# Moving half of one chunk's depthwise convolution from TensorE to VectorE in a fused attention and mixture-of-experts kernel

## The chip, the cores and the metric

The kernel runs on one core of one Trainium2 chip. The metric is device time in microseconds (us) of one execution, from launch to end; the profile gives the span from the first to the last instruction of one such execution. The engines are called PE (TensorE, matmuls), PEld (its weight loads), DVE (VectorE), ACT (ScalarE), POOL (GpSimd) and SP (the queue that issues DMAs). All data are 32-bit floats.

## The reference

The input is 16 images of 256 channels with 64 x 64 pixels. Two layers follow each other, each as a residual.

```python
def layer0(xg):                      # xg: group norm of x, 32 groups
    xn = rmsnorm(xg, g_norm)         # over the channels
    q, k, v = w_qkv @ xn             # 4 heads of 32
    q = softmax(q, over head_dim); k = softmax(k, over pixels)
    context = k @ v.T; out = context.T @ (q * 32 ** -0.5)
    return rmsnorm(w_out @ out + b_out, g_out)

def layer1(xg):                      # xg: group norm of the new x
    prob = softmax((mean over pixels of xg) @ router_w.T / 2)
    for the two best of 4 experts:   # chosen per image, weights sum to 1
        h = gelu(depthwise 3x3 convolution of xg by dw[e] + dw_b[e])
        out += weight * (pw[e] @ h + pw_b[e])
    return out

x = x + layer0(group_norm(x)); x = x + layer1(group_norm(x))
```

## The kernel before

Every image passes through phases: "in" (statistics of the first norm), "q" (norm, transposes, projection, the sums for the attention context), "out" (attention output, its norm, the transpose back and the sum into the image), "route" (second norm, choice of experts) and "x" (the experts). Phases in, q and out run over 8 groups of 512 pixels; x runs over 4 chunks j of 16 rows (1024 pixels). Phases of neighbouring images overlap.

The order of all instructions is written out. Each step is entered with `at(phase, image, group, key, function)`, its place is the phase's start plus the slot times the group plus a number from the table `PLAN`, and all steps are sorted by place and emitted in that order (`rows.sort`, line 917). Each engine takes its instructions strictly in this order. The phase x has slots of 16 places, and one image has 64 places.

In phase x the 256 channels are split into two halves, for which the convolution is done in different ways.

- Channels 128 to 255, "the second half", go by DVE. `pad1` (line 693) writes the normed chunk with its border rows into one of two padded buffers `pd1`; `start1` (line 731) begins an accumulator "acc" on ACT with the first of nine taps; `tap1` (line 739) adds the other eight on DVE, 1024 pixels in one instruction; `gelu1` (line 746) writes the result "h". This is done for both chosen experts. There are two "acc" buffers.
- Channels 0 to 127, "the first half", go by PE. `pad0` (line 653) writes the chunk into `pd0` with even and odd rows and columns apart; `lay` (line 678) copies it to HBM; `spread` (line 683) reads it back so that 16 channels at a time, with their pixel neighbourhood, fill the 128 partitions; `conv0` (line 713) convolves both experts with two matmuls of 256 columns per group of 16 channels, 8 groups; `gelu0` (line 724) evacuates.

`pointwise` (line 752) multiplies by the chosen experts' weights. It fills four PSUM banks per chunk, one for each set q of pixels (even or odd row, even or odd column), and each bank holds two output halves m of 256 pixels. Parts 0 and 1 multiply "h" of the two experts at full depth of 128 (line 768). Parts 2 and 3 multiply the first half's result in four bands of 32 partitions (line 779, "banded")[...]. Part 4, used in the last image alone, adds the image itself by an identity matmul (line 774). `residual` (line 788) adds bank and bias into the image: on DVE (line 795), or on ACT in the last image (line 793), where the image is in the bank already. There are seven PSUM banks for all of this and one more for the context.

Other steps of which the prediction speaks: `out_norm` (line 456) scales the attention output on DVE (line 463), in the last image on ACT (line 461); `out_add` sums it into the image (line 477); `stats` (line 262) takes the first norm's statistics; `gn1_sums` (line 490) has one instruction per image at line 493; `pick_taps` (line 554) chooses the second half's taps; line 241 and 242 are the helper `rsqrt`, begun on DVE and ended on POOL; line 416 is a small matmul of the attention's weights. Two paths exist, and a check on the weights at the start selects the pipelined one (`pipelined_path`), which all traces here run.

Of the kernel before, what the change touches and what calls it, by code (L numbers as in the profile page):

```python
# [47 lines left out]
EARLY = 3  # L48
NRING = 7
# [4 lines left out]
    "load_x1": 2.47, "mean": 1.04, "means": 4.69, "dev": 5.07, "devs": 8.24, "scale": 8.52,  # L54
    "bias": 12.08, "in_lead": 22.23, "norm0": -5.91, "norm1": -3.77, "turn_x0": 0.61, "x_sq0": 1.9,
    "x_sq1": 2.11, "turn_x1": 1.64, "x_sq2": 2.36, "x_sq3": 2.68, "token": 3.59, "x_keep0": 5.41,
    "x_keep1": 5.42, "x_keep2": 5.2, "x_keep3": 5.22, "project0": 3.62, "evacuate0": 5.48,
    "project1": 4.85, "evacuate1": 5.69, "project2": 5.61, "evacuate2": 6.6, "project3": 5.69,
    "evacuate3": 6.83, "context": 7.87, "q_sum": 8.01, "q_norm": 13.4, "q_turn": 15.77,
    "q_keep": 16.04, "mix_a": 8.41, "mix_turn": 9.67, "mix_v": 10.33, "mix_vv": 11.49, "mix_b": 12,  # L60
    "mix_out": 12.87, "mix_c": 13.33, "mix_lead": 15.68, "attend0": -0.16, "out_sq0": 0.33,
    "out_sq1": 0.7, "out_scale0": 1.35, "out_norm0": 2.44, "attend1": 0.39, "out_sq2": 1.3,
    "out_sq3": 1.47, "out_scale1": 2.38, "out_norm1": 3.76, "out_turn0": 4.83, "out_add0": 6.02,
    "sq_sums0": 6.68, "out_turn1": 5.56, "out_add1": 6.85, "sq_sums1": 7.24, "sums1": 7.53,
    "means1": 7.77, "scale1": 8.7, "router": 9.48, "route": 9.99, "choose": 12.08,
    "pick_taps": 16.41, "route_lead": 22.29, "pick_rows0": 12.27, "pick_rows1": 15.38,
    "pick_row_bias": 13.7, "weigh": 19.29, "pick_bias": 20.19, "pick000": 1.5, "pick100": 11.76,
    "pick001": 2.67, "pick101": 11.83, "pick002": 5.78, "pick102": 15.2, "pick003": 8.9,
    "pick103": 15.49, "pick010": 1.98, "pick110": 13.36, "pick011": 3.58, "pick111": 15.09,
    "pick012": 4.61, "pick112": 15.41, "pick013": 6.8, "pick113": 16.18, "lay_pw": 10.27,  # L70
    "spread_pw": 12.95, "taps0": 6.17, "taps1": 1.71, "taps2": 2.27, "taps3": -4.16, "taps4": 9.52,
    "taps5": -1.21, "taps6": -1.21, "taps7": 11.56, "pad1": -10.11, "start0": -3.22, "tap01": 0.77,
    "tap02": 1.13, "tap03": 1.92, "tap04": 2.35, "tap05": 2.68, "tap06": 3.77, "tap07": 5.22,
    "tap08": 6.68, "gelu10": 10.88, "start1": 3.82, "tap11": 5.21, "tap12": 6.65, "tap13": 8.35,
    "tap14": 9.77, "tap15": 11.78, "tap16": 12.05, "tap17": 13.11, "tap18": 13.97, "gelu11": 15.52,
    "pad00": 1.66, "pad01": 2.92, "lay": 4.37, "spread0": 6.43, "conv0": 10.64, "gelu00": 11.57,
    "spread1": 6.19, "conv1": 11.39, "gelu01": 12.09, "spread2": 5.8, "conv2": 10.58,
    "gelu02": 11.06, "spread3": 6.79, "conv3": 12.01, "gelu03": 12.46, "spread4": 6.78,
    "conv4": 13.04, "gelu04": 14.02, "spread5": 7.96, "conv5": 13.16, "gelu05": 14.2,
    "spread6": 9.37, "conv6": 13.42, "gelu06": 14.64, "spread7": 10.33, "conv7": 13.97,  # L80
    "gelu07": 14.66, "pw00": 16.91, "pw01": 17.04, "pw02": 18.17, "pw03": 18.59, "pw10": 19.2,
    "pw11": 20.88, "pw12": 21.41, "pw13": 21.48, "residual00": 20.87, "residual01": 25.47,
    "residual02": 27.17, "residual03": 27.67, "store0": 29.36, "residual10": 23.57,
    "residual11": 25.64, "residual12": 27.45, "residual13": 28.04, "store1": 33.91,
    "in_first": 2.74, "in_more": 1.74, "q_first": 9.11, "out_first": 7.86, "out_more": 15.48,
    "q_less": 0.26, "load_a0": -16.2, "load_a1": -8.65, "load_b0": -17.65, "load_b1": -7.1,
    "stats0": -4.87, "stats1": -3.45, "load_weights": 21.49, "scale_weights": -2.89,
    "spread_taps00": -8.7, "spread_taps01": -1.56, "spread_taps10": 1.5, "spread_taps11": 5.1,
    "end_pw00": 16.45, "end_pw01": 18.13, "end_pw02": 14.45, "end_pw03": 15.46,
    "end_residual00": 23.47, "end_residual01": 25.21, "end_residual02": 26.09,  # L90
    "end_residual03": 28.08, "end_pw10": 17.51, "end_pw11": 19.09, "end_pw12": 14.97,
    "end_pw13": 16.08, "end_residual10": 28.63, "end_residual11": 28.83, "end_residual12": 29.05,
    "end_residual13": 30.35, "x_0": -0.07, "x_1": -0.03, "x_2": -0.04, "x_e1": -0.24, "x_e2": -0.02,
    "route_0": 1.22, "route_1": -0.07, "route_2": 0, "route_e1": 0.66, "route_e2": 0.04,
    "out_0": -0.91, "out_1": 0.05, "out_2": -0.02, "out_e1": 0.4, "out_e2": 0.22, "q_0": -0.72,
    "q_1": 1.29, "q_2": 0.04, "q_e1": -0.03, "q_e2": 0, "in_0": 8.12, "in_1": 4.22, "in_2": 0.93,
    "in_e1": 0.1, "in_e2": 0.11, "pw04": 19.17, "pw14": 23.02, "end_pw04": 18.16, "end_pw14": 20.35,
# [4 lines left out]
def pipelined_path(ctx, tc, ring, wqkv, x, w_outT, b_out, g_out, router_wT, router_b, dw, dw_b, pwT, pw_b, out):  # L102
# [79 lines left out]
    dww = const.tile([P, NE, 10], FP, name="dww")  # L182
# [7 lines left out]
    def load_weights():  # L190
# [5 lines left out]
        nc.sync.dma_start(out=dww[:, :, 0:9], in_=dw[P:C])  # L196
        nc.sync.dma_start(out=dww[:, :, 9:10], in_=dw_b[P:C])
# [63 lines left out]

    def stats(b, g, k):
        st = live["st", b] if ("st", b) in live else new(small, [P, KH, NG, 6], "st", b, bufs=2)
        nc.vector.bn_stats(st[:, k, g], live.pop(("xa", b, g, k)) if b else x1(b, g)[:, k])  # L264
# [191 lines left out]
    def out_norm(b, g, hf):  # L456
        ob = new(work, [P, 2, C], "ob", b, g, hf, bufs=3)
        s, po = live.pop(("s", b, g, hf)), live.pop(("po", b, g, hf))
        if b == NB - 1:
            for c in range(2):  # L460
                nc.scalar.activation(ob[:, c], po[:, c], AF.Copy, scale=s[:, c : c + 1])
        else:
            nc.vector.tensor_tensor(ob, po, s.unsqueeze(2).to_broadcast([P, 2, C]), ALU.mult)
# [90 lines left out]
    def pick_taps(b):  # L554

        oh, ds = live["oh", b], new(small, [P, TOPK, 10], "ds", b, bufs=2)
        for i in range(TOPK):
            dt = new(small, [P, 10, NE], "dt", b, i, bufs=2)
            nc.vector.tensor_tensor(
                dt, dww.rearrange("p e t -> p t e"),  # L560
                oh[:, i].unsqueeze(1).to_broadcast([P, 10, NE]), ALU.mult,
            )
            nc.vector.tensor_reduce(ds[:, i], dt, AX.X, ALU.add)
# [66 lines left out]
    def lay_pw(b):  # L630

        d = live["layp", b] = hbm.tile([P, TOPK * C], FP, tag="layp", name=f"layp_{b}")
        nc.sync.dma_start(out=d, in_=live.pop(("pw0", b)).rearrange("p i o -> p (i o)"))
# [18 lines left out]

    def pad0(b, j, s):
# [11 lines left out]
        if s == 0:  # L665
            if j == 0:
                nc.gpsimd.memset(pd0[:, 0, :, 0], 0.0)
            else:
                nc.gpsimd.tensor_copy(pd0[:, 0, :, 0], pd0[:, 0, :, QA])
        xs = x1c(b, j)[:, 0].rearrange("p (a s w) -> p a s w", s=2, w=W)  # L670
        put(1 - s, s, QA, xs[:, :, s])
# [11 lines left out]
    def spread(b, j, g):  # L683

        d, t = live["lay", b, j], new(work, [P, QA * PC], "xr", b, j, g, bufs=12)
        rows = d[g * CH : (g + 1) * CH].rearrange("c (v n) -> v c n", v=4)
        for a in range(2):
            nc.sync.dma_start(
                out=t[a * P // 2 : (a + 1) * P // 2],
                in_=rows[:, :, a * PC : (a + QA) * PC],  # L690
            )

    def pad1(b, j):

        t, prev = pd1[j % 2], pd1[(j + 1) % 2]
# [17 lines left out]
    def conv0(b, j, g):  # L713
        if g % 2 == 0:
            live["dw", b, j, g // 2] = bank("dw", b, j, g)
        po = live["dw", b, j, g // 2][:, g % 2 * GT // 2 : (g % 2 + 1) * GT // 2]
        rows3 = live["xr", b, j, g].rearrange("p (a w) -> p a w", w=PC)
# [6 lines left out]
    def gelu0(b, j, g):  # L724

        po = live["dw", b, j, g // 2][:, g % 2 * GT // 2 : (g % 2 + 1) * GT // 2]
        nc.scalar.activation(  # L727
            live["xr", b, j, g][:, 0 : GT // 2], po, AF.Gelu, bias=live["bv", b][:, g : g + 1]
        )

    def start1(b, j, i):
        ds = live["ds", b]
        acc = new(work, [P, QR, W], "acc", b, j, i)
        nc.scalar.activation(  # L734
            acc, pd1[j % 2][:, 0:QR, 0:W], AF.Identity,
            bias=ds[:, i, 9:10], scale=ds[:, i, 0:1],
        )

    def tap1(b, j, i, t):
        acc = live["acc", b, j, i]  # L740
        nc.vector.scalar_tensor_tensor(  # L741
            acc, pd1[j % 2][:, t // 3 : t // 3 + QR, t % 3 : t % 3 + W],
            live["ds", b][:, i, t : t + 1], acc, ALU.mult, ALU.add,
# [7 lines left out]

    def pointwise(b, j, m, part):


        ms = slice(m * P, (m + 1) * P)

        both = (b, j) == (NB - 1, NQ - 1)
        if ("ppw", b, j) not in live:
            live["ppw", b, j] = [bank("pw", b, j, q) for q in range(4)]
        group = ("parts", b, j, None if both else m)  # L760
        parts = live[group] = live.get(group, 0) + 1
        n = 5 if b == NB - 1 else 4
# [788 lines left out]
```

## Time and profile before

| what | value |
|---|---|
| median of 3 runs | 2724.32 us (2722.52 to 2724.56) |
| the profiled execution | 2722.39 us |
| its span, first to last instruction | 2720.7 us |
| mean granted TensorE clock | 0.992 |
| PE busy | 2636.2 us, 97% |
| PEld busy | 2257.1 us, 83% |
| DVE busy | 2417.5 us, 89% |
| ACT busy | 2083.4 us, 77% |
| POOL busy | 767.4 us, 28% |
| DMA | 394.77 MB, mean 145 GB/s |

Busy time is the time in which at least one instruction of the engine is recorded as running. Records of successive instructions overlap a little, so what one instruction costs its engine is better read from the start of one to the start of the next. In a row of the profile, `L741 DVE ... acc<-pd,ds,acc` names the line, the engine, and the tiles written and read.

### The profile page before, as it was taken

To read this page: it belongs to the slowest core of one execution; us is meant where nothing else is said; L and a number is where in the kernel's file an instruction comes from. 1 tells how busy PE (TensorE), PEld (TensorE's weight loads), DVE (VectorE), ACT (ScalarE), POOL (GpSimd) and SP (SyncE) were. 2 spreads that over 40 slices of the span, in tenths; PEclk is the share of its full clock that TensorE was granted. 3 is DMA by queue.
4 is the path that set the end of the run, shared out by engine and by line. 5 is a ranking of instruction groups with operands and counts; after the bars stand their busy time and mean duration, and the time that the engine had idled before them with its cause. 6 is when DMAs were issued, how large, how long until landed. Compare 5 with 4: busy or idle time off the path is not lost.

```text
span 2720.7 us, 55294 instructions
## 1 busy us (share of the span) xinstructions
PE 2636.2 (97%) x19300; PEld 2257.1 (83%) x19300; DVE 2417.5 (89%) x4480; ACT 2083.4 (77%) x5230; POOL 767.4 (28%) x874
## 2 busy tenths in 40 slices
PE   6898999999999999999999999999999999998888
PEld 5787888888888888888888888888888888886677
DVE  6889998999989898898989989898898988889984
ACT  3576788887887888788787888888788788876543
POOL 2242232322323222232322323233222323232200
PEclk9999999999999999999999999999999999999989
DMA  4335454454545546355354545445454443525332
GB/s 155 113 125 148 141 170 153 133 167 155 154 146 158 158 144 184 129 162 170 125 170 153 155 155 158 155 143 173 143 159 154 145 135 123 150 85 140 118 110 89
DMA packets 229711, 394.77 MB, mean 145 GB/s; under 512 B 25904, under 2 KB 108336, under 8 KB 229424
## 3 DMA queue, kind: packets, MB, share of 16 engines
q1 hardware_dynamic: 228880, 390.75, 46.4%
q8 instruction: 156, 2.56, 0.4%
q14 instruction: 131, 1.07, 0.1%
q10 hardware_dynamic: 544, 0.39, 0.0%
HBM read 280.82 MB, written 110.23 MB: 144 GB/s over the span
## 4 chain that ended last, share of the span: by engine, by line
PE 88%; DVE 7%; ACT 1%; issue 1%; DMA 1%; POOL 1%; SPq 0%; ACTq 0%; POOLq 0%; DVEq 0%
PE pw L779 17%; PE pw L768 16%; PE dw L719 15%; PE pq L346 14%; PE pc L364 8%; PE po L440 8%; PE px L315 4%; PE tr L468 4%; DVE acc L741 3%; PE ptq L387 2%; DMA ring<-in_x 1%; DVE ring L477 1%; DVE ring L795 1%; PE pw L774 1%; DVE st L264 0%
## 5 line engine op out<-in xcount | busy, mean ns | idle before, releaser
L741 DVE SCALAR_TENSOR_TENSOR acc<-pd,ds,acc 128x1024 f32<-128x1024 f32 x1024 | 1304.7, 1284 | 14.7 <-ACT acc L734 10.9
L242 POOL TENSOR_TENSOR s<-s,mhalf 128x2 f32<-128x2 f32 x256 | 212.2, 831 | 1103.2 <-DVE s L241 1085.4
L346 PE MATMUL pq<-wqkv_n,xg 128*128 128x256 f32 x2048 | 504.7, 384 | 0.9
L719 PE MATMUL dw<-xr,taps 128*128 128x256 f32 x2048 | 489.2, 381 | 8.4 <-ACT xr L727 6.2
L768 PE MATMUL pw<-h,pw 128*128 128x256 f32 x2048 | 480.7, 383 | 15.6 <-ACT h L750 10.0
L779 PE MATMUL pw<-xr,psp 32*128 32x256 f32 x8192 | 485.1, 382 | 0.0
L779 PEld LDWEIGHTS pw<-xr,psp 32*128 32x128 f32 x8192 | 405.9, 185 | 66.7 <-issue 47.3
L768 PEld LDWEIGHTS pw<-h,pw 128*128 128x128 f32 x2048 | 382.2, 191 | 74.3 <-ACT h L750 12.4
L719 PEld LDWEIGHTS dw<-xr,taps 128*128 128x128 f32 x2048 | 374.5, 190 | 58.9 <-ACT xr L727 11.4
L346 PEld LDWEIGHTS pq<-wqkv_n,xg 128*128 128x128 f32 x2048 | 370.8, 192 | 58.2 <-ACT xt L333 11.7
L322 ACT ACTIVATE jx<-px 128x256 f32<-128x256 f32 x512 | 195.3, 381 | 193.6 <-PE px L315 173.9
L354 ACT ACTIVATE e<-pq,r 128x256 f32<-128x256 f32 x512 | 219.8, 470 | 134.5 <-PE pq L346 119.7
L242 POOL TENSOR_TENSOR r<-r,mhalf 128x4 f32<-128x4 f32 x128 | 186.1, 1454 | 448.8 <-DVE r L241 425.5
L795 DVE SCALAR_TENSOR_TENSOR ring<-pw,bs,ring 128x256 f32<-128x256 f32 x480 | 214.5, 475 | 66.1 <-PE pw L768 37.5
L440 PE MATMUL po<-mw,qt 128*128 128x256 f32 x1024 | 253.1, 381 | 0.7 <-DVE ring L795 0.7
L727 ACT ACTIVATE xr<-dw,bv 128x256 f32<-128x256 f32 x512 | 219.5, 478 | 40.1 <-PE dw L719 38.1
L364 PE MATMUL pc<-xt,e 128*128 128x257 f32 x1024 | 245.9, 382 | 3.6 <-DVE xt L331 3.4
L484 ACT ACTIVATE sqj<-ring,nm 128x512 f32<-128x512 f32 x256 | 185.9, 726 | 70.7 <-DVE ring L477 68.9
L477 DVE SCALAR_TENSOR_TENSOR ring<-tr,gout,ring 128x512 f32<-128x512 f32 x256 | 188.8, 746 | 41.5 <-PE tr L468 37.0
L448 ACT ACTIVATE junk<-po 128x256 f32<-128x256 f32 x512 | 196.5, 384 | 25.5 <-PE po L440 20.7
L364 PEld LDWEIGHTS pc<-xt,e 128*128 128x128 f32 x1024 | 189.4, 191 | 29.0 <-issue 3.4
L440 PEld LDWEIGHTS po<-mw,qt 128*128 128x128 f32 x1024 | 190.2, 190 | 28.0 <-issue 2.0
(144 smaller groups left out, 3569.6 us busy)
## 6 DMA issues: line engine op xcount, KB each, us to landing
xr<-lay SPq DMA_DIRECT2D x1024, 66.0 KB
ring<-in_x SPq DMA_DIRECT2D x256, 256.0 KB
out<-ring SPq DMA_DIRECT2D x128, 512.0 KB
xa<-in_x SPq DMA_DIRECT2D x240, 256.0 KB
xb<-in_x SPq DMA_DIRECT2D x240, 256.0 KB
lay<-pd SPq DMA_DIRECT2D x64, 594.0 KB
psp<-layp SPq DMA_DIRECT2D x128, 128.0 KB
layp<-pw SPq DMA_DIRECT2D x16, 256.0 KB
```

The source lines that it names most:

```text
L242: nc.gpsimd.tensor_tensor(out_t, out_t, mhalf[:, :n], ALU.pow)
L346: nc.tensor.matmul(pq, xg[:, k, c * P : (c + 1) * P], wqkv[:, k, : 2 * HID], start=(k == 0), stop=(k == KH - 1),)
L354: nc.scalar.activation(live["e", b, g][:, c], live["pq", b, g, c // 2][:, c % 2], AF.Exp, scale=live["r", b, g][:, c : c + 1],)
L364: nc.tensor.matmul(live["pc", b], live["e", b, g][:, c, HID:], xt[g % 2][:, c], start=(g == 0 and c == 0), stop=(g == NG - 1 and c == CG - 1),
L440: nc.tensor.matmul(po[:, c], qt[:, n * P : (n + 1) * P], live["mw", b], start=True, stop=True)
L477: nc.vector.scalar_tensor_tensor(xin, live.pop(("tr", b, g, k)), gout[:, k : k + 1], xin, ALU.mult, ALU.add, accum_out=live["sm", b][:, 0, ...
L719: nc.tensor.matmul(po, live[f"taps{g}", b][:, d * P : (d + 1) * P], rows3[:, :, d : d + W // 2], start=(d == 0), stop=(d == 1),)
L727: nc.scalar.activation(live["xr", b, j, g][:, 0 : GT // 2], po, AF.Gelu, bias=live["bv", b][:, g : g + 1])
L741: nc.vector.scalar_tensor_tensor(acc, pd1[j % 2][:, t // 3 : t // 3 + QR, t % 3 : t % 3 + W], live["ds", b][:, i, t : t + 1], acc, ALU.mul ...
L768: nc.tensor.matmul(po[q], live["pw1", b][:, part, ms], h[:, q % 2, q // 2], start=begin, stop=end,)
L779: nc.tensor.matmul(po[q], live["psp", b][band, g, ms], live["xr", b, j, g][band, 0 : GT // 2], start=begin and g % 4 == 0, stop=end and g ...
L795: nc.vector.scalar_tensor_tensor(xo, po, bs, xo, ALU.add, ALU.add)
```

## The change

1. In chunk 1 (`REST = 1`) of every image but the last but one, PE convolves only the first four of the eight row pairs of the first channel half. The other eight rows go by DVE: `pad_rest`, `start_rest` (ACT), 16 `tap_rest` of 512 pixels (DVE) and `gelu_rest` (ACT), in one of the two "acc" buffers; the padded buffers `pd1` take turns over five users per image, and four where there is no rest. `conv0`, `gelu0`, `spread` and the banded parts of `pointwise` shrink to half in this chunk, and a new part 5 multiplies the rest at full depth. `pick_taps` chooses taps for both channel halves.
2. `out_norm` of the second half of each group is done on ACT in all images, and all of it in the first and last.
3. `pointwise` opens one accumulation per bank for both output halves, where it opened one for each half.
4. In the last image the identity matmul and ACT residual stay for chunks 0 and 1 alone (`by_pe`).
5. The statistics of the first two pixel groups of image 0 are taken ahead of the branch (`HEAD_STATS = 2`).
6. All numbers of `PLAN` are new, and DVE's convolution has a phase "v" of its own.

```diff
+HEAD_STATS = 2
+REST = 1
 PLAN = {
...
-    dww = const.tile([P, NE, 10], FP, name="dww")
+    dww = const.tile([P, KH, NE, 10], FP, name="dww")
...
-        if b == NB - 1:
+        if hf or b in (0, NB - 1):
             for c in range(2):
                 nc.scalar.activation(ob[:, c], po[:, c], AF.Copy, scale=s[:, c : c + 1])
...
+    def pairs(b, j):
+
+        return QA // 2 if j == REST and b != NB - 2 else QA
+
+    def padded(b, j):
+
+        before = b * NQ + b - (b > NB - 2)
+        if pairs(b, REST) < QA:
+            j = REST + 1 if j == NQ else j + (j > REST)
+        return pd1[(before + j) % 2]
...
-        rows3 = live["xr", b, j, g].rearrange("p (a w) -> p a w", w=PC)
+        n = pairs(b, j)
+        po = live["dw", b, j, g // 2][:, g % 2 * GT // 2 :][:, : n * W // 2]
+        rows3 = live["xr", b, j, g].rearrange("p (a w) -> p a w", w=PC)[:, :n]
...
+    def pad_rest(b):
+        t, xs = padded(b, NQ), x1c(b, REST)[:, 0].rearrange("p (r w) -> p r w", w=W)
+        sck, bik = scale1(b, 0)
+        nc.scalar.activation(
+            t[:, 0 : QA + 1, 1 : W + 1], xs[:, QA - 1 :], AF.Identity, bias=bik, scale=sck
+        )
+        nc.scalar.activation(
+            t[:, QA + 1, 1 : W + 1], x1c(b, REST + 1)[:, 0, 0:W], AF.Identity, bias=bik, scale=sck
+        )
+
+    def start_rest(b, i):
+        ds = live["ds", b][:, 0, i]
+        if i == 0:
+            new(work, [P, QR, W], "acc", b, NQ)
+        nc.scalar.activation(
+            live["acc", b, NQ][:, i * QA : (i + 1) * QA], padded(b, NQ)[:, 0:QA, 0:W],
+            AF.Identity, bias=ds[:, 9:10], scale=ds[:, 0:1],
+        )
+
+    def tap_rest(b, i, t):
+        acc = live["acc", b, NQ][:, i * QA : (i + 1) * QA]
+        nc.vector.scalar_tensor_tensor(
+            acc, padded(b, NQ)[:, t // 3 : t // 3 + QA, t % 3 : t % 3 + W],
+            live["ds", b][:, 0, i, t : t + 1], acc, ALU.mult, ALU.add,
+        )
+
+    def gelu_rest(b, i):
+        acc = live["acc", b, NQ][:, i * QA : (i + 1) * QA]
+        nc.scalar.activation(acc, acc, AF.Gelu)
+
+    def parts(b, j):
+
+        return [0, 1, 2, 3] + [4] * by_pe(b, j) + [5] * (pairs(b, j) < QA)
...
-        both = (b, j) == (NB - 1, NQ - 1)
...
-        begin, end = parts == 1, parts == (n * KH if both else n)
+        done = live["parts", b, j] = live.get(("parts", b, j), 0) + 1
+        begin, end = done == 1, done == KH * len(parts(b, j))
...
+        elif part == 5:
+            for i in range(TOPK):
+                h = live["acc", b, NQ][:, i * QA : (i + 1) * QA]
+                h = h.rearrange("p (a o) (c t) -> p t o a c", o=2, t=2)
+                for q in range(4):
+                    nc.tensor.matmul(
+                        po[q][:, n:], live["pw0", b][:, i, ms], h[:, q % 2, q // 2],
+                        start=begin and i == 0, stop=end and i == TOPK - 1,
+                    )
+        else:
+            for g in range(4 * part - 8, 4 * part - 4):
+                for q in range(4):
+                    band = slice(q * P // 4, (q + 1) * P // 4)
+                    nc.tensor.matmul(
+                        po[q][:, :n], live["psp", b][band, g, ms], live["xr", b, j, g][band, :n],
+                        start=begin and g % 4 == 0, stop=end and g % 4 == 3,
+                    )
+
+    def by_pe(b, j):
+
+        return b == NB - 1 and j < NQ // 2
...
-        if b == NB - 1:
+        if by_pe(b, j):
             nc.scalar.activation(xo, po, AF.Identity, bias=bs)
...
+            if pairs(b, j) < QA:
+                at("v", b, j, "pad_rest", pad_rest, b)
+                for i in range(TOPK):
+                    at("v", b, j, f"start_rest{i}", start_rest, b, i)
...
+    st_0 = head.tile([P, KH, NG, 6], FP, name="st_0")
...
+        for g in range(HEAD_STATS):
+            for k in range(KH):
+                nc.vector.bn_stats(st_0[:, k, g], ring[g // 2][:, k, g % 2])
```

## The prediction

> **What bounds the kernel now.** I read the share of busy time by engine first, then busy time by stage, then the matmuls in order of time, then what VectorE waits for.
>
> ```profile
> PE 2636.2 (97%) x19300; PEld 2257.1 (83%) x19300; DVE 2417.5 (89%) x4480; ACT 2083.4 (77%) x5230; POOL 767.4 (28%) x874
> ```
>
> ```profile
> 0.00:340.00 340.00, 292.67 (x1773) 249.77 (x1777) 292.26 (x678) 209.34 (x618) 105.24 (x136) 0.97 0.43 136
> 340.00:2380.00 2040.00, 2039.08 (x15110) 1756.91 (x15103) 1849.69 (x3391) 1683.02 (x4189) 596.82 (x667) 1.00 0.50 153
> 2380.00:2550.00 170.00, 157.89 (x1223) 129.32 (x1222) 152.37 (x255) 118.08 (x289) 48.30 (x49) 1.00 0.39 121
> 2550.00:2721.00 171.00, 146.61 (x1204) 121.05 (x1202) 123.20 (x159) 72.91 (x136) 17.02 (x23) 0.94 0.30 97
> ```
>
> The columns after the stretch are PE, PEld, DVE, ACT, POOL. From 340 to 2380 us PE is busy 2039 of 2040 us; the 84 us it is idle lie at the two ends. A busy PE could still be slow inside, so I check the pace of single passes. An fp32 matmul is recorded as two passes.
>
> ```profile
> 1327.75 3.62 PE L719 MATMUL dw<-xr,taps 128*128 128x256 f32 x16
> 1331.20 0.60 PE L468 MATMUL tr<-ident,ob 128*128 128x128 f32 x4
> ...
> 1340.81 3.74 PE L779 MATMUL pw<-xr,psp 32*128 32x256 f32 x64
> 1344.48 0.66 PE L387 MATMUL ptq<-ident,e 128*128 128x128 f32 x4
> ```
>
> From one group's start to the next, 16 passes of 256 columns take 3.45 us: 216 ns each. 64 passes of the four 32-row bands take 3.67 us; four run side by side, so that is 16 steps of 216 ns plus 0.21 us. Entering such a run costs about 0.1 us more, so a banded run costs some 0.3 us beyond its streaming.
>
> One image's period comes from line 493, which runs once per image: it starts at 1295.38 and next at 1457.58, **162.2 us per image**. At that pace DVE's 1849.69/2040 (90.7%) is 147.1 us per image, idle 15.1; ACT's 82.5% is 133.8.
>
> ```profile
> DVE s L241 <- ACT junk L448: 36.6, 29, 2.5
> DVE ring L795 <- PE pw L768: 32.4, 26, 2.1
> DVE ring L477 <- PE tr L468: 31.9, 37, 1.0
> DVE ring L795 <- PE pw L779: 23.7, 25, 1.2
> ```
>
> These four waits in 340 to 2380 us (total, times, longest) say why DVE idles: it arrives before PE or ACT has finished. Such waits shrink by themselves when DVE is later. PE shows no wait at all there.
>
> [...] The trace has the narrow case, two matmuls of 128 columns at full depth:
>
> ```profile
> 171.70 0.61 PE L416 MATMUL pv<-cx,wqkv_n 128*128 128x128 f32 x4
> 172.14 0.60 PE L468 MATMUL tr<-ident,ob 128*128 128x128 f32 x4
> ```
>
> Four passes in 0.44 us, 110 ns each, which is half of 216: the load does not spoil it. [...] at 1321.86 a load is followed by its ACTIVATE at 1323.15, 1.29 us later, so I price a load at 1.3.
>
> **The change, part by part.** In 15 of 16 images half of chunk 1 of channels 0 to 127 leaves PE's convolution.
>
> PE, per such image:
> - Convolution: 8 groups x 2 column shifts x 2 passes = 32 passes shrink from 216 to 110 ns: -3.4 us.
> - Banded pointwise: 2 output halves x 8 groups x 2 passes = 32 four-band steps shrink likewise: -3.4 us. No banded step of 128 columns is in this trace; bounds: 110 ns (as line 416) or 216 (no gain, +3.4 us). I take 110, since four bands together stream like one.
> - Part 5: 2 halves x 2 experts x 4 pixel sets x 2 passes = 32 new passes x 110 ns: +3.5 us.
> - One accumulation per bank: the instruction order has 122 banded runs against 149; 27 x 0.3 us over 15 images: -0.6 us.
>
> Sum **-3.9 us: 158.3 per image**. In the last image the identity matmuls of two chunks go: 2 x 8 x 2 passes x 216 ns = -6.9 us, once.
>
> DVE, per image, priced by spacing, since records overlap:
>
> ```profile
> 1304.36 0.68 DVE L463 TENSOR_TENSOR ob<-po,s 128x512 f32<-128x512 f32 x1
> 1304.97 0.47 DVE L795 SCALAR_TENSOR_TENSOR ring<-pw,bs,ring 128x256 f32<-128x256 f32 x1
> 1305.36 2.47 DVE L741 SCALAR_TENSOR_TENSOR acc<-pd,ds,acc 128x1024 f32<-128x1024 f32 x2
> ```
>
> A 1024-element tap is spaced 2.47 - 1.28 = 1.19 us, a 256-element one 0.39, so 512 elements come to 0.39 + 0.8/3 = 0.66 (bounds 0.61, the spacing of line 463[...]). 16 taps: +10.5 us. Eight output norms leave: -8 x 0.61 = -4.9. The wider tap choice adds 0.1. DVE becomes 147.1 + 5.7 = **152.8 us, 96.5% of 158.3**: its idle room falls from 15.1 to 5.5 us. The last image also gets 16 residuals back, 16 x 0.39 = 6.2 us.
>
> ACT, per image:
>
> ```profile
> 1316.81 1.55 ACT L333 ACTIVATE xt<-px,r 128x256 f32<-128x256 f32 x4
> ...
> L307 ACT ACTIVATE xg<-xb,bi,sc 128x512 f32<-128x512 f32 x208 | 169.4, 814 | 0.0
> ```
>
> Norms 16 x 0.39 = 6.2; two starts at 0.75 and two gelus at 0.65, 2.8; pads of 576 and 64 elements, 1.1; 27 more table loads by the instruction order (137 against 110), 27 x 1.3/16 = 2.2; halved gelus and pads -1.3. ACT becomes 133.8 + 11.0 = 144.8 (91%). That lies beside PE while ACT is ahead; if the cover is gone, evacuations come late and PE waits for banks.
>
> New waits: the rest's accumulator is one of the two "acc" buffers, so chunk 2's second start on ACT waits for the last part-5 matmul of chunk 1, and whatever ACT has queued behind it waits too. Four statistics move ahead of the branch: DVE may wait there for the first image loads, with the branch itself queued behind; 0 to +1 us, against 4 x 0.68 = 2.7 us saved later; I take 0. POOL loses 15 copies and the SP queue has 2 more small weight loads and 240 halved spreads: nothing, both are idle most of the time. The reworked order cannot be summed from any row; I bound it by the idle room above.
>
> Sum: I let the tighter DVE and ACT cost PE 0.8 us per image, a choice: 159.1. The saturated pace holds for 13 images (line 493 starts from 322 to 2430): 13 x 3.1 = 40 us. Start: 0, since PE idles there anyway. Tail: PE saves up to 3.9 + 6.9 = 10.8 us, DVE gains 16.7 us of work there but idles 171 - 123 = 48 us after 2550; I take -4. The profiled execution took 2722.4 us (span 2720.7 and 1.7 around it), 1.9 under the median 2724.3. 2722.4 - 44 = 2678; with the median's offset **2680 us**.
>
> **The rivals.**
> - Forecast, 0.66: PE sets a shorter pace, 2655 to 2705. 2655: no new idle time (13 x 3.9 + 11 + start 5); 2705: 2 us more idle per image than I chose.
> - DVE becomes the bound, slower, 0.20. Place: the DVE queue, where 16 taps stand between chunk 1 and the residuals that free PE's banks. Its 15.1 us of waits stay: 147.1 + 5.7 + 15.1 = 167.9 us, +5.7 x 13 = 74, 2797 us. It decides once more than 162.2 - 152.8 = 9.4 of the 15.1 us stay. For: in-order queues, ACT at 91% too. Against: all four waits are of an early DVE.
> - Banded steps do not shrink at 128 columns: +3.4 x 15 = 51 us, 2731. 0.06. Against: the 110 ns row.
> - No gain: ordering eats 3 us per image, about 2722. 0.08.
>
> **How the numbers follow.** A measurement of this kernel can tell about 0.2%, 5.4 us, from no change. The no-gain case splits into 0.03 faster and 0.05 same, the banded one into 0.02 same and 0.04 slower: faster 0.66 + 0.03, same 0.05 + 0.02, slower 0.20 + 0.04. The range 2655 to 2735 takes in the forecast, no gain, banded and the edge of the DVE case; most of that case and a larger gain stay out. The forecast's own range is 2655 to 2705.
>
> **What would show it.** Right: line 493's successor every 159 us; 240 half convolutions at 110 ns a pass; PE still without waits; DVE near 96%. Wrong: PE waiting for DVE's residuals, taps or ScalarE's gelu in mid-run, or banded steps of 128 columns above 110 ns.

## The result and the profile after

The change makes the kernel slower: **2783.2 us** (median of 4 runs, 2780.98 to 2787.9) against 2723.4 for the kernel before in the same comparison, a ratio of 1.0221 (95% interval 1.0208 to 1.0234). The profiled execution took 2784.26 us, its span is 2782.5.

The shares of busy time by engine, of the kernel after:

```profile
PE 2618.4 (94%) x19764; PEld 2250.0 (81%) x19764; DVE 2566.1 (92%) x4608; ACT 2227.9 (80%) x5588; POOL 911.6 (33%) x859
```

PE does less (2618 against 2636 us) in a longer span; DVE and ACT do more, in the direction foretold. Busy time from 340 to 2380 us, after (columns PE, PEld, DVE, ACT, POOL; then the granted TensorE clock, the busy share of the DMA engines and GB/s):

```profile
340.00:2380.00 2040.00, 1981.37 (x15253) 1713.98 (x15245) 1930.11 (x3431) 1766.18 (x4389) 713.06 (x647) 1.00 0.47 146
```

In this stretch PE was idle for 1 us before; now it is idle for 2040 - 1981.4 = 58.6 us. The granted clock in this stretch is 1.00 in both kernels, so it is not the clock. The pace is again read from the instruction that runs once per image, line 493 before and line 504 now, in the timeline of DVE after:

```profile
1328.91 0.18 DVE L504 TENSOR_REDUCE s<-sm 128x4 f32<-128x32 f32 x1
...
1494.14 0.18 DVE L504 TENSOR_REDUCE s<-sm 128x4 f32<-128x32 f32 x1
```

This image takes 165.2 us; the mean over the 13 intervals of the saturated stretch is 165.5, where it was 162.1 (both means are over the starts of the same instruction). So of the 61.8 us that the span grew, 13 x 3.4 = 44 lie there; the interval ahead of them grew by 7.7, the one behind them by 8.7, and what follows the last by 1.8.

What PE waits for from 340 to 2380 us, after (total, times, longest, in us); before, this list was empty:

```profile
PE px L326 <- ACT xr L758: 9.7, 12, 0.9
PE dw L749 <- DMA xr<-lay: 9.4, 10, 2.9
PE dw L749 <- ACT jx L333: 7.5, 10, 0.8
PE pq L357 <- DVE ring L877: 7.0, 12, 0.7
PE tr L479 <- ACT xt L344: 6.9, 11, 0.7
PE pw L836 <- DVE ring L488: 4.1, 10, 0.4
PE pt L416 <- DVE cn L410: 3.8, 11, 0.9
PE pz L538 <- DVE ob L474: 3.8, 8, 0.5
```

The stretch holds 12.3 images, so each of these waits comes about once per image, and none is long. Six of the eight, 39 of the 58 us, name a releaser that produces nothing the waiting matmul reads, but reads a PSUM bank: `px` waits for the gelu that reads a `dw` bank, `pq` for the residual that reads a `pw` bank. Read so, they are waits for a free bank. Only the second (the spread's data) and the seventh (the context) are waits for data. The profile infers the releaser that an entry names, so it is the pattern that counts: many small waits, no large one.

### The profile page after: what moved, and what is told of

The parts are those of the page before. It is cut to its first block, busy times and chain, and to the rows that moved or that the text cites. A ratio compares the mean times of both kernels' runs of the same rounds, so it can differ in the third digit from the quotient of the medians.

```text
span 2782.5 us, 56901 instructions
## 1 busy us (share of the span) xinstructions
PE 2618.4 (94%) x19764; PEld 2250.0 (81%) x19764; DVE 2566.1 (92%) x4608; ACT 2227.9 (80%) x5588; POOL 911.6 (33%) x859
## 4 chain that ended last, share of the span: by engine, by line
PE 56%; DVE 25%; issue 6%; ACT 5%; POOL 4%; DMA 3%; SPq 1%; DVEq 0%; ACTq 0%; POOLq 0%
PE pw L836 11%; DVE acc L771 11%; PE pw L857 10%; PE pq L357 9%; PE dw L749 7%; PE po L451 5%; PE pc L375 5%; DMA xr<-lay 3%; PE tr L479 2%; PE px L326 2%; DVE acc L804 2%; DVE ring L877 2%; DVE st L275 2%; PE pw L849 2%; DVE ring L488 2%
## 5 line engine op out<-in xcount | busy, mean ns | idle before, releaser
L771 DVE SCALAR_TENSOR_TENSOR acc<-pd,ds,acc 128x1024 f32<-128x1024 f32 x1024 | 1339.2, 1311 | 8.1 <-ACT acc L765 3.9
L251 POOL TENSOR_TENSOR s<-s,mhalf 128x2 f32<-128x2 f32 x256 | 310.1, 1212 | 1333.4 <-DVE s L250 1267.6
L749 PE MATMUL dw<-xr,taps 128*128 128x256 f32 (+1 forms) x2048 | 452.6, 364 | 55.3 <-DMA xr<-lay 40.7
L836 PE MATMUL pw<-h,pw 128*128 128x256 f32 (+1 forms) x2064 | 476.9, 383 | 4.9 <-DVE ring L488 4.1
L749 PEld LDWEIGHTS dw<-xr,taps 128*128 128x128 f32 x2048 | 355.8, 194 | 113.5 <-issue 28.3
L857 PE MATMUL pw<-xr,psp 32*128 32x256 f32 (+1 forms) x8192 | 426.4, 356 | 0.0
L857 PEld LDWEIGHTS pw<-xr,psp 32*128 32x128 f32 x8192 | 368.7, 185 | 36.3 <-issue 19.0
L251 POOL TENSOR_TENSOR r<-r,mhalf 128x4 f32<-128x4 f32 x128 | 203.1, 1587 | 196.8 <-DVE r L250 195.4
L758 ACT ACTIVATE xr<-dw,bv 128x256 f32<-128x256 f32 (+1 forms) x512 | 215.5, 478 | 61.5 <-PE dw L749 51.8
L344 ACT ACTIVATE xt<-px,r 128x256 f32<-128x256 f32 x416 | 169.6, 506 | 80.4 <-POOL r L251 80.3
```

The source lines that it names most:

```text
L251: nc.gpsimd.tensor_tensor(out_t, out_t, mhalf[:, :n], ALU.pow)
L749: nc.tensor.matmul(po, live[f"taps{g}", b][:, d * P : (d + 1) * P], rows3[:, :, d : d + W // 2], start=(d == 0), stop=(d == 1),)
L758: nc.scalar.activation(live["xr", b, j, g][:, :n], po, AF.Gelu, bias=live["bv", b][:, g : g + 1])
L771: nc.vector.scalar_tensor_tensor(acc, padded(b, j)[:, t // 3 : t // 3 + QR, t % 3 : t % 3 + W], live["ds", b][:, 1, i, t : t + 1], acc, AL ...
L836: nc.tensor.matmul(po[q][:, lo:hi], live["pw1", b][:, part, ms], h[:, q % 2, q // 2, lo * 2 // W : hi * 2 // W], start=begin and lo == 0, ...
L857: nc.tensor.matmul(po[q][:, :n], live["psp", b][band, g, ms], live["xr", b, j, g][band, :n], start=begin and g % 4 == 0, stop=end and g % ...
```

## The experiments

All ratios are to the kernel before, with the 95% interval. "Pace" is the mean of the same 13 intervals. Gains in us are differences of medians. The intervals of e1, h3 and h1 overlap with that of the kernel after, so their gains of 3 to 5 us are at the edge of what can be told apart. Theories: **DVE** has become the bound; **ACT** evacuates too late; **POOL** or the **SP queue** delays someone; or the **order** itself, whatever the load, no longer fits. DVE, ACT, PE and SP do keep to the order: after the branch, all 4219 instructions of DVE, 3840 of ACT and 2105 DMAs of SP in the trace before, and 4343, 4170 and 2107 in the one after, start in the order in which the kernel emits them, as far as the tiles that they write and read tell; so do PE's runs of passes, 1896 before and 1873 after.

### Is it the load of one engine?

**e1** takes 12 of the 16 new taps per image away from the kernel after:

```diff
-                    for t in range(1, 9):      # tap_rest
+                    for t in (1, 2):
```

> The changed kernel, but only 2 of the 8 DVE taps of each rest are added (24 instead of... 4 of 16 instructions per image stay; the remaining taps of those eight rows are left out of the computation). DVE loses 12 x 0.66 = 7.9 us per image, everything else stays. If DVE's load sets the pace: PE's own pace of about 158.5 to 160 us per image comes back, 13 to 15 images x 5.5 us less than 2783: about 2700 to 2712. If the new order with its latencies on ACT, POOL and DMA sets it: 2760 or more. If ACT's load sets it: 2775 to 2785.

Measured: 2777.95 us, 1.0199 (1.0182 to 1.0216), pace 165.45. Busy time by stage, e1:

```profile
340.00:2380.00 2040.00, 1983.08 (x15220) 1714.17 (x15216) 1826.85 (x3291) 1765.90 (x4391) 704.59 (x646) 1.00 0.48 146
```

DVE's busy time falls from 1930 to 1827 us, below the 1850 of before, and the kernel gains 5 us of 60, hardly any of it in the pace (165.45 against 165.52). DVE's load is not the bound.

**h3** makes ACT's square sums of the second norm light:

```diff
-            junk, x1(b, g)[:, k], AF.Square, ...
+            junk[:, :64], x1(b, g)[:, k, :64], AF.Square, ...
```

> The changed kernel with the second norm's sums of squares on ACT taken over 64 of the 512 pixels of each group (the rest of that sum is left out, so the second norm and all after it are off): ACT loses 16 x 0.47 = 7.5 us per image, nothing moves. If ACT's load makes PE's suppliers late: the pace falls by 3 to 5 us per image, 2710 to 2745. If the order alone counts, as for DVE in e1: 2765 to 2785.

Measured: 2778.98 us, 1.02 (1.0183 to 1.0217), pace 165.38. Busy time by stage, h3:

```profile
340.00:2380.00 2040.00, 1981.30 (x15239) 1715.72 (x15232) 1931.23 (x3436) 1702.77 (x4392) 713.07 (x646) 1.00 0.48 146
```

ACT's busy time falls by 63 us in this stage, most of what the change had added (83), and PE's idle time is the same to 0.1 us. The load of ACT alone is not it.

**f1 and f2** concern something that I had not priced. The costliest groups show POOL's power step for the scale `s` of the output norm longer, first before, then after:

```profile
L242 POOL TENSOR_TENSOR s<-s,mhalf 128x2 f32<-128x2 f32 x256 | 212.2, 831 | 1103.2 <-DVE s L241 1085.4
```

```profile
L251 POOL TENSOR_TENSOR s<-s,mhalf 128x2 f32<-128x2 f32 x256 | 310.1, 1212 | 1333.4 <-DVE s L250 1267.6
```

831 ns on the average became 1212. The timeline of POOL after shows two lengths:

```profile
1314.66 1.59 POOL L251 TENSOR_TENSOR s<-s,mhalf 128x2 f32<-128x2 f32 x1 [10.97 <-DVE s L250]
1318.59 0.69 POOL L251 TENSOR_TENSOR s<-s,mhalf 128x2 f32<-128x2 f32 x1 [2.34 <-DVE s L250]
```

VectorE's taps at these times:

```profile
1314.42 1.27 DVE L771 SCALAR_TENSOR_TENSOR acc<-pd,ds,acc 128x1024 f32<-128x1024 f32 x1
1318.75 1.28 DVE L771 SCALAR_TENSOR_TENSOR acc<-pd,ds,acc 128x1024 f32<-128x1024 f32 x1
```

The long step begins while a tap runs and ends 0.56 us after the tap's end. The short one begins before the next tap does, and that tap doesn't lengthen it. This holds throughout: 150 of the 256 steps after begin in a tap, and each of them takes 1.06 us or more; none of the others takes over 0.80. The records show the size, 0.7 against 1.6 us, but not how a tap lengthens a step. Before, only 36 of the steps begin in a tap; in e1, where 12 of the 16 new taps are gone, 138 still do. It is the new order, not the new taps, that brings the two together. Taps are lengthened in their turn: the new ones of 512 pixels last 1.14 us on the average beside POOL's product `e` (128 x 512, 25 of them), and 0.75 us where POOL is idle. f1 drops the power of `s` and `r` from the kernel after, f2 from the kernel before:

```diff
...
-        nc.gpsimd.tensor_tensor(out_t, out_t, mhalf[:, :n], ALU.pow)
+        if power:                       # False for s and r
+            nc.gpsimd.tensor_tensor(out_t, out_t, mhalf[:, :n], ALU.pow)
```

> The changed kernel without the POOL step of the two token scales (the power -1/2 of the sums 'r' and 's' is left out, so the scales are wrong); nothing else moves. POOL theory: these steps take 1.6 to 2.0 us instead of 0.7 to 1.0 when a VectorE tap stands behind them, ACT's context copies and norms wait for them (97 us in 340 to 2380) and hold up everything behind them: the pace falls from 165.2 to about 159 to 161, 2700 to 2725. If only the order of PE, ACT and DVE counts: within 15 us of 2783.

> The kernel before without the same POOL step, the control. POOL theory: 2710 to 2722, since there ACT waits for POOL only 22 us in 340 to 2380 and PE never waits. If the POOL step costs both kernels alike: 2665 or less.

Measured: f1 2773.28 us, 1.0182 (1.0165 to 1.0199), pace 164.84; f2 2727.73 us, 1.0014 (1.0007 to 1.0021). Taking the steps away gains 10 us in the kernel after and nothing in the one before. A real part, about a sixth of the loss.

**h1** gives the loads of the statistics their old places:

```diff
-    "load_a0": -12.88, "load_a1": -18.45,
+    "load_a0": -16.2, "load_a1": -8.65,
```

> The changed kernel with the places of the two statistics loads (load_a0, load_a1) of the kernel before. In the changed order SP waits 403 us in 340 to 2380 for a free statistics tile, which it never did before, and the spreads stand behind. If that queue is a main cause: the convolution's waits (28.7 us against 6.8 in that stretch) go, and some 1.5 to 2 us per image: 2755 to 2765. If it is a side effect: 2775 to 2785.

The reason to try it is what the SP queue waits for in the same stage, after:

```profile
SPq L266 <- DVE st L275: 402.6, 130, 6.8
```

A load that waits for a free tile stops the queue: it stood over 0.1 us ahead of 153 of the 181 statistics loads in this stage, and after 29 of these the next issue was a spread. Measured: 2779.89 us, 1.0204 (1.0187 to 1.0221), pace 165.37. The entry is gone from h1's list, but the queue then stands longer at another place (399 instead of 217 us for the padded `pd`), PE's waits for the spreads fall only from 9.4 to 6.6 us, and the time by 3 us: a side effect.

**i1** makes the cuts of e1, f1 and h3 at once, in case each is masked by the others.

> The changed kernel with the three cuts of e1, f1 and h3 at once (4 of 16 rest taps, no power on POOL for the two token scales, sums of squares over 64 of 512 pixels; these parts of the computation are left out). If the loads act together: PE sets the pace again at 158 to 160 us per image, 2690 to 2715. If the banks or the order alone count: no more than the sum of the three single gains, 5 + 10 + 4 = 19 us, so 2760 to 2780.

Measured: 2763.06 us, 1.0152 (1.0135 to 1.0169), pace 164.5. Busy time by stage and some of PE's waits, i1:

```profile
340.00:2380.00 2040.00, 1993.03 (x15234) 1726.03 (x15231) 1827.55 (x3305) 1712.41 (x4425) 311.97 (x350) 1.00 0.48 147
```

```profile
PE dw L750 <- DMA xr<-lay: 11.2, 10, 2.1
PE px L327 <- ACT xr L759: 8.1, 12, 0.8
PE pq L358 <- DVE ring L878: 4.6, 11, 1.0
```

The gain is 20 us, the sum of the three alone (5 + 10 + 4): they do not act together. DVE now stands at 89.6% and ACT at 83.9%, where the kernel before has 90.7 and 82.5, and POOL far below. With nearly the loads of before, and less work on PE than before, 40 us of loss are left, with waits at mostly the same places. That they are due to the order is what remains when the loads are out; the small edits that came with it are in i1 too.

### Is it one part of the change?

**e4 and e4b** take the rest away from the kernel after: PE convolves all rows again, the order stays. e4 left the formula that alternates the padded buffers as it was, which then counts five users for four; e4b mends that.

```diff
-        return QA // 2 if j == REST and b != NB - 2 else QA
+        return QA
...
-        before = b * NQ + b - (b > NB - 2)
+        before = b * NQ                 # e4b only
```

> The changed kernel without the rest: PE convolves all rows again, the new order of steps and the split norms stay. PE +3.4 us per image (155.4 us of streaming, as before), DVE -10.5. If DVE's load sets the pace: PE sets it again at about 162 us, 2715 to 2735. If the new order sets it: 2770 to 2800.

> The changed kernel without the rest, as in e4, with the two padded buffers alternating over four users per image (in e4 the first chunk of the next image was padded into the buffer that the last taps still read, which left those rows wrong and made taps and pads wait for each other). PE +3.4 us per image, DVE -10.5. If DVE's load sets the pace: 2715 to 2735. If the new order with its latencies sets it: 2765 to 2800, because the steps stand in the same places.

**e5** is the kernel before with the second edit alone:

```diff
-        if b == NB - 1:
+        if hf or b in (0, NB - 1):
```

> The kernel before with half of the output norms (all in image 0) on ACT, nothing else: DVE -4.9 us per image, ACT +6.2. If ACT had room, 2715 to 2728. If ACT is the engine that comes too late once it is loaded: 2740 to 2790.

Measured: e4 2804.83 us, 1.0298 (1.0281 to 1.0316); e4b 2788.46 us, 1.0243 (1.0226 to 1.026), pace 166.36; e5 2732.21 us, 1.003 (1.0019 to 1.0042), pace 162.77. Busy time by stage, e4b and then e5:

```profile
340.00:2380.00 2040.00, 1996.73 (x14752) 1719.85 (x14748) 1783.04 (x3220) 1706.85 (x4276) 700.18 (x656) 1.00 0.48 149
```

```profile
340.00:2380.00 2040.00, 2038.03 (x15088) 1748.89 (x15087) 1800.22 (x3277) 1742.72 (x4378) 597.22 (x666) 1.00 0.51 152
```

e4b and e5 share the norms on ACT and have no rest; DVE and ACT are busy for no larger share of the time in e4b. They differ by the numbers of `PLAN`, the one accumulation, `by_pe`, the early statistics, the wider tap choice and two small tiles (`st`, `dt`) with one buffer instead of two, and by 56 us. In e5 PE is still full, in e4b it idles 43 us. The first three of its waits:

```profile
PE dw L749 <- DMA xr<-lay: 15.0, 11, 2.0
PE dw L749 <- ACT jx L333: 6.9, 10, 0.7
PE tr L479 <- ACT xt L344: 6.4, 10, 0.7
```

With `pt` (4.6 us) and `pz` (3.9) these are five of the eight places of the kernel after, 36.8 us here and 31.4 there. The other three of that list, `px` for the gelu, `pq` for the residual and `pw` for `out_add`, 20.8 us, come to 0.4 us in e4b: they come with the rest. So **a loss of the same size is there in the new order before the convolution moves**, and the moved convolution changes the sum little (2788.5 to 2783.2, the intervals of the ratios overlap). It does not show that the two losses are the same one: the new order came with work taken off PE, and in e4b PE has that work back.

**e2 and e3** put the norms back on DVE, or all of them on ACT, in the kernel after:

```diff
-        if hf or b in (0, NB - 1):
+        if b == NB - 1:                 # e2; e3: if True:
```

> The changed kernel with all output norms on DVE as before (last image on ACT): DVE +4.9 us per image, ACT -6.2. If DVE's load sets the pace: slower by up to 4.9 x 14, about 2835 to 2850. If ACT's load: faster, about 2700 to 2720. If the order: within 15 us of 2783.

> The changed kernel with all output norms on ACT: DVE -4.9 us per image, ACT +6.2 (to about 149 of 165 us). If DVE's load sets the pace: faster by 3 to 4.9 us per image, about 2715 to 2740. If ACT's load: slower, about 2850. If the order: within 15 us of 2783.

Measured: e2 2817.3 us, 1.0345 (1.0328 to 1.0363), pace 167.45; e3 2882.13 us, 1.0583 (1.0561 to 1.0605), pace 173.36. The same move costs 8 us in the old order (e5) and is worth 34 us in the new one (e2). A move has no price of its own here; it has one for each order. This holds for e4b as well.

### Is it one part of the order?

**g1, g2, g3** start from e4b (with the one accumulation undone in g1 and g3) and give groups of steps their old places: g1 all of phase x, g2 all but phase x, g3 the pointwise, residual and store steps. In g3 some steps then read other values than the reference's; the instructions are those of e4b. **i2** moves two numbers of the kernel after, so that the first pointwise part opens its banks later:

```diff
-    "pw00": 17.45, ... "pw10": 17.45,
+    "pw00": 20.46, ... "pw10": 20.47,
```

> e4b (no rest, new order, split norms) with the places of phase x (pads, spreads, convolution, pointwise, residuals, picks) and its slots taken from the kernel before, each output half its own accumulation again; all other phases keep the new places. If the new x order alone costs the time, of which the longer hold of the four pointwise banks is one part: 2725 to 2745. If the other phases' new places cost it: 2775 or more.

> e4b with the places of all phases but x taken from the kernel before; phase x keeps the new places and one accumulation per bank. If the new x order costs the time: 2775 to 2800. If the other phases' places do: 2725 to 2745. If it is neither alone: between.

> e4b with the places of the pointwise parts, residuals and stores alone taken from the kernel before (each output half its own accumulation). The trace shows the four banks held for 34.7 us per chunk in e4b and 31.7 in the kernel before, in which the other steps share the three that are left. If the bank hold is the cause: the hold falls to about 32 us and the time to 2725 to 2750. If the spreads and convolutions come too late in the new order: 2770 or more.

> The changed kernel with one edit of the order: the first pointwise part (pw00, pw10) is placed at 20.46 and 20.47 instead of 17.45, just ahead of the next one, so that the four banks are opened some 3 places, about 7 us, later and closed as before. If the bank hold is the cause: the hold falls from 35.0 to about 28 us and the time by 20 to 45 us, to 2740 to 2765. If it is not: within 8 us of 2783, or slower since PE has less to do while banks fill.

Measured: g1 3034.96 us, 1.1143 (1.1125 to 1.1162); g2 3163.79, 1.1605 (1.1579 to 1.1631); g3 2993.73, 1.0991 (1.0973 to 1.101); i2 2934.54, 1.0768 (1.075 to 1.0786), pace 176.58. The time from the first pointwise matmul of a chunk to its last residual, for which it holds four of the seven banks, is in the trace 31.7 us before, 35.0 after, 36.6 in g3 and 30.7 in i2. i2 did what it was meant to do, shorten the hold, and lost 151 us. PE's waits from 340 to 2380 us, i2:

```profile
PE pc L324 <- ACT e L314: 91.8, 82, 2.8
```

This wait does not exist in the kernel after: the pointwise passes that were moved had probably covered the time in which ACT makes `e` for the context matmul. The granted clock in this stretch also fell where the loss is large: 0.97 in g1, 0.93 in g2, 0.99 in g3, 0.98 in i2, so the waits are not all of it. Mixing two orders is far worse than either, and for that reason these runs do not tell which group of the new order costs the 60 us.

### Does the moved work pay in the old order?

**f4** adds the moved work (the rest and the norms, edits 1 and 2) to the old order, without edits 3 to 5, with the 16 taps spread over 20 places and buffers of their own for the rest. Their room comes from other tiles: `xa` 2 instead of 3, `xr` 11 instead of 12, `ob` 2 instead of 3, `qt` 8 instead of 9.

> The change's work in the order of the kernel before: rest on VectorE with its own padded buffer and accumulator (so that its 16 taps can be spread thinly over 20 places of chunks 0 and 1 and none stand in a row), half of the norms on ACT, each half its own accumulation, identity matmuls in all of the last image, one buffer less of xr, xa, ob and qt to make room. If only the order was at fault: PE's 3.3 us per image come out, 8 us for the norms as in e5 go off: 2685 to 2705. If the work itself leaves DVE or ACT too little room: 2740 or more.

Measured: 3066.71 us, 1.1266 (1.1247 to 1.1285). What the SP queue and PE wait for from 340 to 2380 us, f4:

```profile
SPq L216 <- DVE st L225: 695.8, 69, 17.0
```

```profile
PE dw L696 <- DMA xr<-lay: 165.8, 102, 4.9
```

This tells of my buffers, not of the change: with two `xa` tiles the statistics loads stop the SP queue for 696 us, and the convolution waits for the spreads behind them; the granted clock in the stretch is 0.96. **f4b** gives `xa` its third tile back (`xr` is 10); **f5b** is the kernel before with the smaller `xr`, `ob` and `qt` alone.

> As f4, the change's work in the order of the kernel before with the rest's taps spread thinly, but all three statistics tiles kept; room comes from 10 instead of 12 xr, 2 instead of 3 ob and 8 instead of 9 qt. SP is no longer held by the statistics tiles. If the order was at fault and the work pays: 2685 to 2710. If DVE and ACT have no room for it whatever the order: 2735 or more.

> The kernel before with the same smaller rings (10 xr, 2 ob, 8 qt), the control of f4b: 2720 to 2730 if each ring still covers its longest use; what it is above 2723 is to be taken off f4b.

Measured: f4b 2802.48 us, 1.0288 (1.0271 to 1.0305), pace 167.05; f5b 2729.3 us, 1.0019 (1.0012 to 1.0026). The largest of PE's waits in the stage, f4b:

```profile
PE pw L784 <- ACT xt L293: 31.8, 12, 2.7
```

The room costs 5 us, the rest of the 78 is the work at the places that I gave it. Once per image PE waits 2.7 us for ACT's evacuation `xt`. In the trace ACT has one of the new norms in front of it, but in the one that I followed (1253.88 us) it also stands idle itself, 0.70 us for DVE's accumulator and 0.45 us for POOL's power, so this is a chain over three engines and not ACT's load alone. My places for the new steps were one guess among many, so this does not show that the work cannot pay in the old order, only that it doesn't pay for the asking. No version that I ran beats the kernel before.

## Why the prediction was wrong

**Right, in kind and mostly in size.** The half convolutions and half banded passes shrink. In the timeline of PE after:

```profile
1276.15 1.50 PE L749 MATMUL dw<-xr,taps 128*128 128x128 f32 x12
...
1291.88 2.96 PE L857 MATMUL pw<-xr,psp 32*128 32x128 f32 x96
1294.77 2.09 PE L849 MATMUL pw<-acc,pw 128*128 128x128 f32 x16
1296.70 0.61 PE L326 MATMUL px<-ident,xg 128*128 128x128 f32 x4
```

12 passes of a half convolution are recorded in 1.50 us, 125 ns each. 96 passes in four bands are 24 steps in 2.89 us, 120 ns a step with the entry into the run; part 5's 16 passes take 1.93 us, 120 ns each against 110 in the sum. The rival "banded steps do not shrink" falls. A rest tap is spaced 0.66 us, as priced, where nothing disturbs it, in the timeline of DVE after:

```profile
1276.00 0.74 DVE L804 SCALAR_TENSOR_TENSOR acc<-pd,ds,acc 128x512 f32<-128x512 f32 x1
1276.66 0.48 DVE L877 SCALAR_TENSOR_TENSOR ring<-pw,bs,ring 128x256 f32<-128x256 f32 x1
```

DVE came to 1930.11 / 2040 x 165.2 = 156.3 us per image (priced 152.8) and ACT to 143.0 (144.8); start to start, a rest start took 0.71 us, a rest gelu 0.54 and a table load 1.29 (medians), priced at 0.75, 0.65 and 1.3. DVE's 3.5 us too much are mostly taps: over the 13 intervals, start to start without recorded idle time, a rest tap took 0.72 us (11.5 instead of 10.5 per image), and the 64 old taps 80.1 us per image against 78.0 before.

**The step that failed** is the sentence that the reworked order could not be summed and was bounded by the idle room of DVE and ACT, with 0.8 us of idle PE per image as a choice. Idle room of an engine bounds nothing about the order: it says how much work fits, not whether each result is there when PE's queue comes to it. Measured per image: PE idles 58.6 / 12.35 = 4.7 us instead of 0.8, and is busy 1981.4 / 2040 x 165.2 = 160.4 us instead of 158.3. Those two, 3.9 and 2.1, take the predicted 159.1 to 165.1. (In the sum, 27 x 0.3 us over 15 images is 0.5 us, not 0.6; nothing hangs on it.) The idle part is the list of small waits. Of the busy part some 1.2 us lie in the narrow passes, which the sum had at 110 ns: over the 13 intervals, start to start without recorded idle time, a half convolution's pass took 122, one of part 5 120, and a narrow step of four bands 125 ns, 32 of each per image. Most of the rest lies in passes that did not change: the transposes `px` took 121 ns instead of 115, the full-depth pointwise passes 223 instead of 219. Whether the passes are slower or hold waits too short for the list, the records do not tell. e4b against e5 shows that the order, with the small edits that go with it, can lose as much without the convolution moved; i1 shows that two thirds of the loss stay at nearly the loads of before. That the order is what failed is thus the reading that is left; it is not shown by an order that works.

**POOL and the SP queue** were priced at nothing because both are idle most of the time. The idle share was the wrong measure: POOL's short steps became longer (f1, 10 us), while the SP queue's new wait is worth 3 us at most (h1).

**The start and the end** were also mis-sized: 0 and -4 were priced. The span shows +7.3 up to the saturated stretch and 8.7 + 1.8 = +10.5 behind it. Together with 13 x (165.5 - 159.1) = 83 this is the whole error of 103 us, within 2. In e1 the two are +4.8 and +7.3: its 5 us lie here, and what lengthens the start and the end beyond the new taps was not tried.

**The rival of the right sign had the wrong mechanism.** "DVE becomes the bound" gave 2797 us, near the result, but rested on DVE's load, and e1 takes that load away for 5 us; that it came near is chance. What it said of residuals that free PE's banks is in the waits (`pq <- ring`, 7.0 us), as one of many places. The "no gain" case named the mechanism that is left, an order that eats the gain, at 3 us per image; with the slower passes it was 165.5 - 159.1 = 6.4, and I had given it no side on which it goes past zero.

**Open:** which of the numbers of `PLAN` do it, and how much is due to the one accumulation (no run shows what it allows), `by_pe` or the two small tiles (`st`, `dt`) that lost their second buffer, which were not tried alone. The bank waits suggest the longer hold, but i2 shortened it and lost for another reason, so that the hold is the cause is argued, not shown.

## What to carry to other kernels

When one engine is at 97% and all queues are in order, a sum of moved work is only half a forecast: if the order is rewritten as well, price it as an unknown with both signs and let it, not the sum, set the range. Before believing that a busier engine is the bound, cut its load alone and look whether the waits move; here three cuts at once (DVE, ACT and POOL) left 40 of 60 us. And price an edit in the order in which it will run: the same move of norms cost 8 us in one order and was worth 34 in the other.

## What was not expected of the hardware

- A tiny POOL instruction (128 x 2) takes 0.7 us, or 1.6 us if it begins while a tap of VectorE runs; a 128 x 4 one 1.0 or up to 2.0. The order decides how often they meet: the mean went from 831 to 1212 ns, and leaving these steps out gains about 10 us (f1).
- One tile fewer in a ring of loads cost 264 us (f4 against f4b) where the loads share a DMA queue with others: the SP queue of f4 stood 696 us for it, and PE 166 for what was queued behind.
- Moving two of some 250 places by 3 costs 151 us (i2), mostly through one wait of 92 us that was not there before.
